# A key projection moved ahead of the scores, another projection behind the maxima's transposes, and context pieces loaded one batch earlier

## The chip, the cores and the metric

One NeuronCore of one Trainium2 chip runs the kernel; everything is float32. The metric is the device time of one execution in microseconds (us), taken as the median of several runs. The engines are named as the profile names them: PE (TensorE, the matmuls), PEld (its weight loads), DVE (VectorE), ACT (ScalarE), POOL (GpSimd) and SP (the queue that issues the DMAs).

## What is computed

A Perceiver-like block over `x` of 32 batches x 64 rows x 256, with a context of 32 x 1601 x 256:

```python
x = x + cross_attention(layernorm(x), ctx, ctx, mask)   # 16 heads of 16, softmax over 1601 keys
x = x + span_attention(layernorm(x))                    # softmax of -soft * (pos - mean)^2 over 64 rows
x = x + ffn(layernorm(x))                               # shared gated product + 2 of 8 experts per row
```

The cross attention makes nearly all of the work: for every batch the keys and values of 1601 context rows are projected (256 x 256 each), scores of 16 heads are formed against 64 queries, masked, made into a softmax with its true maximum, and multiplied with the values.

## The kernel before

**Units of work.** A batch's heads are handled in two *halves* of eight heads; half number n is batch b = n // 2, c = n % 2, and there are 64. The loop at line 767 runs over n and overlaps four things that belong to different halves: the scores of half n+1, the softmax of half n, the products with the values of half n-1, and the projection of the keys and values of batch b+1. The 1601 keys are cut into 13 blocks of 124. Context comes in four pieces (`GROUPS`: blocks 0-3, 4-6, 7-9, 10-12; five buffers `ct`, line 146), and scores in three *bursts* (`SCORED`: 4, 5 and 4 blocks).

**Operations of one half, as they stand in the loop.**
- `values(n-1, r)` (line 636, tile `pvs`): 104 small matmuls for r = 0, and 104 for r = 1. r = 0 needs the exponentials of pairs 0 and 1 of half n-1, r = 1 those of pairs 2 and 3.
- `exponentials(n, j)` (line 626, ACT, 124 x 1664): one for each of the four pairs of heads. The fourth, of pair 3, is written in the following half: `exponentials(n-1, 3)` at line 789, ahead of `scores(n+1, 0)`.
- `scores(n+1, g)` (line 549, tile `psc`): a burst into four banks (five for g = 1). DVE adds the mask on the way out (lines 566 and 573) and keeps running maxima (line 590; the first of them is an ACT copy, line 582, `mrun`).
- The maxima of half n: `turned_maxima` transposes them on PE (line 597, tile `pm`, behind the first burst of scores), DVE reduces them (line 604, tile `mc`, between its second and third addition of that burst), `maxima_along_rows` broadcasts them on PE (line 612, tile `pb`), and ACT copies them out (line 616, tile `mb`).
- `less_maxima(n, j)` (line 621, POOL): subtracts `mb` from each of the four pairs, 124 x 1664 each. The exponential of a pair needs it.
- `project_keys(b+1, c, g)` (tile `pk`, copied out by ACT at line 510 with the bias) for the four pieces g, and `project_values(b+1, u)` (tile `pv`, copied out by ACT at line 527) for seven units u of two blocks (the last of one). `tiled` splits a product into strips of 32 output columns (line 495), which leaves the sum of the work as it is.
- Small steps of the query projection and of the span attention are fed in by `run(...)` from an agenda; a set of them serves two batches, so four halves make one round.

**What sets the order.** PE, DVE, ACT and POOL execute their instructions in the order in which the code writes them (`manual_schedule`, line 733), each engine waiting at the head of its queue; SP issues DMAs in written order as well. Nearly all PE outputs of the loop come from one pool of six PSUM banks (`ps_x`, line 395, tag `mm`), which are taken in turn: a tile gets the bank of the tile six allocations before it, and its first matmul waits until that tile has been read out. In the kernel before, the allocations from the first burst on are `psc` x4, `pm`, `pk` of piece 0, `pb`, then those of the steps, `psc` x5, `pk` of piece 1, and so on.

`load_context(b+1)` (line 483) issues all four pieces of the next batch, and an `x` tile for even b, at the start of half c = 0.

Of the kernel before, what the change touches and what calls it, by code (L numbers as in the profile page):

```python
# [33 lines left out]
GROUPS = [(0, 4), (4, 3), (7, 3), (10, 3)]  # L34
# [56 lines left out]
def perceiver_kernel(ctx: ExitStack, tc: tile.TileContext, a: dict[str, bass.AP], out: bass.AP):  # L91
    nc = tc.nc
    B = a["ctxT"].shape[0]
    NT = B * S
    NTILE = NT // P
# [12 lines left out]
    def mm_bank(name: str):  # L108
        return ps_mm.tile([P, 512], F32, tag="mm", name=name)
# [16 lines left out]
    def load_x(t: int):  # L126
        xs[t] = work.tile([P, D], F32, tag="x", bufs=5, name=f"x{t}")
        nc.sync.dma_start(out=xs[t], in_=a["x"][t * P : (t + 1) * P, :])
# [14 lines left out]
    def load_piece(b: int, g: int):  # L143
        c0, n = GROUPS[g]
        k0, kn = c0 * CHUNK, min(n * CHUNK, KEYS - c0 * CHUNK)
        ct = big.tile([P, 2, 4 * CHUNK], F32, tag="ct", bufs=5, name=f"ct_{b}_{g}")
        nc.sync.dma_start(
            out=ct[:, :, :kn],
            in_=a["ctxT"][b].rearrange("(c p) k -> p c k", p=P)[:, :, k0 : k0 + kn],
        )  # L150
        cts[b].append(ct)
# [269 lines left out]
    def pair_of(n: int, j: int):  # L421
        return prob[:CHUNK, place(n, j // 2), j % 2]

    def block_of(n: int, k: int):

        first, last = place(n, 0), place(n, 1)
        return prob[:CHUNK, first : last + 1 : last - first, :, k, :]
# [52 lines left out]

        nc.gpsimd.tensor_tensor(xs[t], xs[t], bo_row, ALU.add)

    def load_context(b: int):
        for g in range(len(GROUPS)):
            load_piece(b, g)
        if b % 2 == 0 and b // 2 + 1 < NTILE:
            t = b // 2 + 1
            load_x(t)


    def product(out, lhsT, rhs, start: bool, stop: bool, tiled: bool):
        n = lhsT.shape[-1]
        for at in range(0, n, 32) if tiled else (0,):
            end = min(at + 32, n) if tiled else n
            nc.tensor.matmul(  # L495
                out[at:end], lhsT=lhsT[:, at:end], rhs=rhs, start=start, stop=stop,
                **(dict(tile_position=(0, at)) if tiled else {}),
            )
# [15 lines left out]
    def project_values(b: int, u: int, tiled: bool = False):  # L514

        blocks = range(2 * u, min(2 * u + 2, NKC))
        ps = mm_bank(f"pv_{b}_{u}")
        for n, k in enumerate(blocks):
            g = max(g for g in range(len(GROUPS)) if GROUPS[g][0] <= k)
            k0, kn = (k - GROUPS[g][0]) * CHUNK, min(CHUNK, KEYS - k * CHUNK)  # L520
            for i in range(2):
                product(
                    ps[:kn, n * D : (n + 1) * D], cts[b][g][:, i, k0 : k0 + kn], wvT[:, i, :],
                    i == 0, i == 1, tiled,
                )
        n = len(blocks)
        nc.scalar.copy(  # L527
            vs[b % 2][:kn, 2 * u : 2 * u + n, :, :DK],
            ps[:kn, : n * D].rearrange("p (n h d) -> p n h d", n=n, d=DK),
        )  # L530

    def scores(n: int, g: int, then=None, order=None):

        b, c = halves[n]
        c0, nb = SCORED[g]


        more = [mm_bank(f"psc_{b}_{c}_{g}"), spare_pvs] if nb == 5 else None
        pss = [mm_bank(f"psc_{b}_{c}_{g}_{j}") for j in range(4)]
        for r in range(nb):  # L540
            for j in range(4):
                e, s = divmod(j, 2)[::-1]
                fifth = nb == 5 and r == 4 * s
                i = 4 if fifth else r - (nb == 5 and s == 0)
                ps, at = (more[e], s) if fifth else (pss[j], i)
                if fifth and j == 2:
                    tc.add_manual_dep(nc.tensor.nop().ins, mm.ins.name, IN_TURN, reason="banks")
                k0 = (c0 + i) * CHUNK
                product = nc.tensor.matmul(  # L549
                    ps[:CHUNK, at * P : (at + 1) * P],  # L550
                    lhsT=kTs[c][32 * j : 32 * j + 32, k0 : k0 + CHUNK],
                    rhs=qbd[b // 2][32 * j : 32 * j + 32, c, b % 2, :, :],
                    start=True, stop=True, tile_position=(32 * j, 0),
                )
                if fifth and j == 1:
                    mm = product
        held = then() if then else None
        for item in (order or ORDER[g]).split():
            if item == "t":
                if held is not None:  # L560
                    maxima_of_rows(*held)
            elif item[0] == "m":
                maximum(n, int(item[1:]))
            elif item in "AB":
                k, e = c0 + 4, "AB".index(item)
                nc.vector.tensor_tensor(  # L566
                    block_of(n, k)[:, :, e, :],
                    more[e][:CHUNK, : 2 * P].rearrange("p (r q) -> p r q", r=2),
                    madd_fifth[:CHUNK, None, :].to_broadcast([CHUNK, 2, P]), ALU.add,
                )  # L570
            else:
                j = int(item)
                nc.vector.tensor_tensor(  # L573
                    pair_of(n, j)[:, c0 : c0 + 4, :].rearrange("p k (e q) -> p k e q", e=2),
                    pss[j][:CHUNK].rearrange("p (k e q) -> p k e q", k=4, e=2),
                    madd[:CHUNK, c0 : c0 + 4, None, :].to_broadcast([CHUNK, 4, 2, S]), ALU.add,
                )
# [6 lines left out]
    def maximum(n: int, k: int):  # L584

        dst = mrun
        if k == NKC - 1:
            dst = mxs[n] = work.tile([P, 4, P], F32, tag="mx", bufs=1, name="mx")
        dst, run = (m[:CHUNK].rearrange("p (r i) q -> p r i q", r=2) for m in (dst, mrun))
        nc.vector.tensor_tensor(dst, block_of(n, k), run, ALU.max)  # L590
# [11 lines left out]
    def maxima_of_rows(ps, col):  # L602

        nc.vector.tensor_reduce(  # L604
            col, ps[:, : 4 * CHUNK].rearrange("p (j k) -> p j k", j=4), AX.X, ALU.max
        )
# [18 lines left out]
    def exponentials(n: int, j: int):  # L625
        nc.scalar.activation(pair_of(n, j), pair_of(n, j), AF.Exp)  # L626
# [134 lines left out]
    next(queries, None)  # L761
    for u in range(7):
        project_values(0, u)
    last = len(halves) - 1

    extra = {3 * last - 3: (0,), 3 * last - 2: (1, 2, 4), 3 * last - 1: (5, 6)}
    for n, (b, c) in enumerate(halves[:-1]):
        if c == 0 and b + 1 < B:
            load_context(b + 1)
        if c and b % 2 == 0 and b // 2 + 1 < NTILE:  # L770
            agenda[3 * n].append((b // 2 + 1, query_steps(b // 2 + 1)))

        def project(f, *args):
            if b + 1 < B:
                f(b + 1, *args)

        def steps(g: int):
            run(3 * n + g)
            for u in extra.get(3 * n + g, ()):
                linear_factor(u)  # L780

        def taken_off():
            turned.extend(turned_maxima(n))
            return turned

        turned: list = []
        if n:
            values(n - 1, 0)
            exponentials(n - 1, 3)
        scores(n + 1, 0, taken_off)  # L790
        project(project_keys, c, 0)
        m = maxima_along_rows(turned[1])
        less_maxima(n, 0, m, nc.gpsimd)
        held = 3 * n in held_at
        if not held:
            first_maxima(n + 1)
        run(3 * n)
        if n:
            values(n - 1, 1)
            if c == 0:  # L800
                agenda[3 * n + 1].append((b // 2, finish_steps(b - 1, 3 * n + 1)))
        for u in extra.get(3 * n, ()):
            linear_factor(u)
        if held:
            first_maxima(n + 1)
        else:
            for k in (1, 2) if c else (1, 2, 3):
                maximum(n + 1, k)

        scores(n + 1, 1, order=LATER if held else None if c else SOONER)  # L810
        exponentials(n, 0)
        project(project_keys, c, 1)
        for u in (4, 5) if c else (0, 1):
            project(project_values, u)
        less_maxima(n, 1, m, nc.gpsimd)
        steps(1)
        exponentials(n, 1)

        less_maxima(n, 2, m, nc.gpsimd)
        scores(n + 1, 2)  # L820
        project(project_keys, c, 2, True)
        project(project_keys, c, 3, True)
        for u in (3, 6) if c else (2,):
            project(project_values, u, True)
        less_maxima(n, 3, m, nc.gpsimd)
        exponentials(n, 2)
        steps(2)
# [176 lines left out]
```

## Time and profile before

| | us |
|---|---|
| median of 3 runs (1519.32, 1520.34, 1524.4) | 1520.34 |
| span of the profiled execution, first to last instruction | 1515.7 |
| PE busy / POOL busy in it | 1465.0 / 1120.7 |
| DVE busy / ACT busy in it | 1225.5 / 946.9 |
| first `pm` of the loop to the last | 41.04 to 1347.68 |
| one `less_maxima` on POOL / one `exponentials` on ACT (means) | 3.75 / 1.59 |
| one copy of keys out of `pk` (124 to 496 columns, mean) | 0.585 |

The profiled execution's own time is its span; the profile holds no other time of it, and the median of the separate runs lies 4.6 us above the span. Busy time is the union of an engine's instructions; matmuls overlap, so a busy PE may still be held up inside. Idle time is put down to the instruction whose semaphore came last.

### The profile page before, as it was taken

To read this page: it belongs to the slowest core of one execution; us is meant where nothing else is said; L and a number is where in the kernel's file an instruction comes from. 1 tells how busy PE (TensorE), PEld (TensorE's weight loads), DVE (VectorE), ACT (ScalarE), POOL (GpSimd) and SP (SyncE) were. 2 spreads that over 40 slices of the span, in tenths; PEclk is the share of its full clock that TensorE was granted. 3 is DMA by queue.
4 is the path that set the end of the run, shared out by engine and by line. 5 is a ranking of instruction groups with operands and counts; after the bars stand their busy time and mean duration, and the time that the engine had idled before them with its cause. 6 is when DMAs were issued, how large, how long until landed. Compare 5 with 4: busy or idle time off the path is not lost.

```text
span 1515.7 us, 62949 instructions
## 1 busy us (share of the span) xinstructions
PE 1465.0 (97%) x28600; PEld 1066.5 (70%) x28600; DVE 1225.5 (81%) x2332; ACT 946.9 (62%) x1727; POOL 1120.7 (74%) x508
## 2 busy tenths in 40 slices
PE   8999999999999999999999999999999999998899
PEld 5677767777777767777777777676777677654587
DVE  4889898998989898989989898988899898873100
ACT  3565657676767657576766677575767566766411
POOL 1777787888878887878888888878788788852710
PEclk9999999999999999999999999999999999999999
DMA  5111111111111101111111111011111111005200
GB/s 174 37 45 46 46 47 46 36 50 50 50 50 50 49 25 41 47 53 37 49 50 50 50 50 49 24 43 46 54 37 48 50 50 33 3 9 160 60 29 29
DMA packets 52076, 73.82 MB, mean 49 GB/s; under 512 B 3812, under 2 KB 51040, under 8 KB 51680
## 3 DMA queue, kind: packets, MB, share of 16 engines
q1 hardware_dynamic: 50992, 69.00, 14.9%
q8 instruction: 225, 3.69, 1.0%
q10 hardware_dynamic: 816, 0.79, 0.2%
q14 instruction: 43, 0.35, 0.1%
HBM read 65.57 MB, written 4.19 MB: 46 GB/s over the span
## 4 chain that ended last, share of the span: by engine, by line
PE 76%; DVE 17%; ACT 4%; issue 2%; POOL 0%; DMA 0%; ACTq 0%; DVEq 0%; POOLq 0%
PE pk L495 20%; PE pv L495 19%; PE psc L549 10%; PE pvs L636 10%; DVE mrun L590 8%; DVE prob L573 6%; PE py L934 4%; PE pm L597 2%; PE u L665 2%; PE ph L916 2%; PE pb L612 2%; ACT qbd L474 1%; PE psa L357 1%; PE pq L466 1%; PE po L377 1%
## 5 line engine op out<-in xcount | busy, mean ns | idle before, releaser
L621 POOL TENSOR_TENSOR prob<-prob,mb 124x1664 f32<-124x1664 f32 x252 | 939.0, 3751 | 224.2 <-ACT mb L616 218.8
L573 DVE TENSOR_TENSOR prob<-psc,madd 124x512 f32<-124x512 f32 x768 | 504.0, 680 | 76.5 <-PE psc L549 76.0
L626 ACT ACTIVATE prob<-prob 124x1664 f32<-124x1664 f32 x256 | 406.9, 1591 | 185.0 <-POOL prob L621 182.0
L590 DVE TENSOR_TENSOR mrun<-prob,mrun 124x512 f32<-124x512 f32 x704 | 486.7, 691 | 33.9 <-ACT mrun L582 20.1
L495 PE MATMUL pk<-ct,wkT_sb 128*32 128x372 f32 (+1 forms) x2512 | 387.6, 489 | 8.9 <-DMA wkT_sb<-in_wkT 5.5
L495 PE MATMUL pv<-wvT_sb,ct 128*124 128x256 f32 x3524 | 381.0, 379 | 0.9 <-DVE prob L566 0.8
L495 PEld LDWEIGHTS pv<-wvT_sb,ct 128*124 128x124 f32 x3524 | 272.8, 132 | 110.4 <-issue 17.5
L549 PE MATMUL psc<-qbd,kT 32*124 32x128 f32 x6400 | 241.8, 279 | 8.3 <-issue 6.9
L495 PEld LDWEIGHTS pk<-ct,wkT_sb 128*32 128x32 f32 (+1 forms) x2512 | 148.9, 127 | 140.1 <-issue 95.5
L549 PEld LDWEIGHTS psc<-qbd,kT 32*124 32x124 f32 x6400 | 201.9, 181 | 41.8 <-issue 20.8
L636 PE MATMUL pvs<-prob,v 124*17 124x64 f32 x13312 | 213.6, 220 | 3.0 <-issue 2.8
L527 ACT COPY v<-pv 124x512 f32<-124x512 f32 (+1 forms) x224 | 124.5, 556 | 146.5 <-PE pv L495 146.1
L636 PEld LDWEIGHTS pvs<-prob,v 124*17 124x17 f32 x13312 | 196.0, 98 | 27.9 <-issue 15.7
L510 ACT ACTIVATE kT<-pk,cols 128x372 f32<-128x372 f32 (+2 forms) x256 | 145.7, 585 | 70.0 <-PE pk L495 69.7
L323 ACT ACTIVATE sc<-sc,least 128x64 f32<-128x64 f32 x256 | 85.8, 343 | 2.6 <-DVE least L319 2.5
L936 DVE SCALAR_TENSOR_TENSOR ot<-py,prob 128x256 f32<-128x256 f32 x16 | 6.8, 424 | 75.7 <-PE py L934 66.1
L665 PE MATMUL u<-xfT,sw_sb 128*128 128x512 f32 x128 | 60.9, 624 | 3.6 <-ACT prob L692 2.7
L582 ACT COPY mrun<-prob 124x512 f32<-124x512 f32 x64 | 38.2, 596 | 37.3 <-DVE soft L306 34.3
L612 PEld LDWEIGHTS pb<-cst,mc 128*124 128x124 f32 x256 | 29.4, 135 | 36.6 <-DVE mc L604 30.0
L549 PE MATMUL pvs<-qbd,kT 32*124 32x128 f32 x256 | 54.9, 294 | 0.0
L597 PE MATMUL pm<-cst,mx 124*128 124x124 f32 x256 | 41.4, 283 | 11.4 <-DVE mx L590 10.1
L323 ACT ACTIVATION_READ_ACCUMULATOR sc<-sc,least 128x1 f32 x256 | 49.9, 195 | 0.0
(126 smaller groups left out, 1220.3 us busy)
## 6 DMA issues: line engine op xcount, KB each, us to landing
ct<-in_ctxT SPq DMA_DIRECT2D x64, 372.0 KB, 3.2
ct<-in_ctxT SPq DMA_DIRECT2D x32, 496.0 KB, 5.1
ct<-in_ctxT SPq DMA_DIRECT2D x32, 361.0 KB, 3.9
w<-in_w SPq DMA_DIRECT2D x16, 256.0 KB, 7.0
x<-in_x SPq DMA_DIRECT2D x16, 128.0 KB, 2.1
x_kept<-x SPq DMA_DIRECT2D x16, 128.0 KB, 2.0
prob<-x_kept SPq DMA_DIRECT2D x8, 256.0 KB, 6.3
out<-ot SPq DMA_DIRECT2D x16, 128.0 KB, 1.9
```

The costliest lines, as they stand in the source:

```text
L323: nc.scalar.activation(sc[:, h, :], sc[:, h, :], AF.Exp, bias=least[:, h : h + 1], scale=-1.0, accum_out=total[:, h : h + 1],)
L495: nc.tensor.matmul(out[at:end], lhsT=lhsT[:, at:end], rhs=rhs, start=start, stop=stop, **(dict(tile_position=(0, at)) if tiled else {}),)
L510: nc.scalar.activation(kTs[c][:, k0 : k0 + kn], ps[:, :kn], AF.Identity, bias=cols[:, B_K + c : B_K + c + 1])
L527: nc.scalar.copy(vs[b % 2][:kn, 2 * u : 2 * u + n, :, :DK], ps[:kn, : n * D].rearrange("p (n h d) -> p n h d", n=n, d=DK),)
L549: product = nc.tensor.matmul(ps[:CHUNK, at * P : (at + 1) * P], lhsT=kTs[c][32 * j : 32 * j + 32, k0 : k0 + CHUNK], rhs=qbd[b // 2][32 * j ...
L573: nc.vector.tensor_tensor(pair_of(n, j)[:, c0 : c0 + 4, :].rearrange("p k (e q) -> p k e q", e=2), pss[j][:CHUNK].rearrange("p (k e q) -> ...
L590: nc.vector.tensor_tensor(dst, block_of(n, k), run, ALU.max)
L597: nc.tensor.transpose(ps[:, j * CHUNK : (j + 1) * CHUNK], m[:CHUNK, j, :], ident[:CHUNK, :CHUNK])
L621: engine.tensor_tensor(sj, sj, m[:CHUNK, j, None, :].to_broadcast([CHUNK, NKC, P]), ALU.subtract)
L626: nc.scalar.activation(pair_of(n, j), pair_of(n, j), AF.Exp)
L636: nc.tensor.matmul(pvs[32 * j : 32 * j + DK + 1, c, :, r, :], lhsT=v[:kn, k, 8 * c + h, :], rhs=pair_of(n, h // 2)[:kn, k, (h % 2) * S : ( ...
L665: nc.tensor.matmul(ps, lhsT=w[:, c, hc * P : (hc + 1) * P], rhs=xfT[:, c, :, slot], start=(c == 0), stop=(c == 1),)
```

## The change

Three edits in the loop. (1) The keys' piece 0 is projected ahead of the first burst of scores, tiled, instead of behind it untiled. (2) Behind the transposes of the maxima stands another unit: for c = 0 the keys' piece 1, for c = 1 the unit 3 of the values. The units after it move up accordingly: piece 2 of the keys goes from the third part of the half (tiled) to the second (untiled), and unit 5 of the values from the second part (untiled) to the third (tiled). (3) The four pieces of a batch are no longer issued together at c = 0 of the batch before it; each is issued one batch earlier still, behind the work that frees its buffer. The pieces of batch 1 are issued ahead of the loop.

```diff
-    def load_context(b: int):
-        for g in range(len(GROUPS)):
+    def piece_ahead(b: int, g: int):
+        if b < B:
             load_piece(b, g)
-        if b % 2 == 0 and b // 2 + 1 < NTILE:
-            t = b // 2 + 1
-            load_x(t)
...
+    for g in range(len(GROUPS)):
+        load_piece(1, g)
     last = len(halves) - 1
...
-        if c == 0 and b + 1 < B:
-            load_context(b + 1)
+        if c == 0:
+            piece_ahead(b + 2, 0)
+            if b % 2 == 0 and b // 2 + 1 < NTILE:
+                load_x(b // 2 + 1)
...
         if n:
             values(n - 1, 0)
             exponentials(n - 1, 3)
+        project(project_keys, c, 0, True)
+        if c:
+            piece_ahead(b + 2, 1)
         scores(n + 1, 0, taken_off)
-        project(project_keys, c, 0)
+        if c:
+            project(project_values, 3)
+        else:
+            project(project_keys, c, 1)
         m = maxima_along_rows(turned[1])
         less_maxima(n, 0, m, nc.gpsimd)
...
         scores(n + 1, 1, order=LATER if held else None if c else SOONER)
         exponentials(n, 0)
-        project(project_keys, c, 1)
-        for u in (4, 5) if c else (0, 1):
-            project(project_values, u)
+        if c:
+            project(project_keys, c, 1)
+            piece_ahead(b + 2, 2)
+            project(project_values, 4)
+            project(project_keys, c, 2)
+            piece_ahead(b + 2, 3)
+        else:
+            project(project_keys, c, 2)
+            for u in (0, 1):
+                project(project_values, u)
         less_maxima(n, 1, m, nc.gpsimd)
...
         less_maxima(n, 2, m, nc.gpsimd)
         scores(n + 1, 2)
-        project(project_keys, c, 2, True)
         project(project_keys, c, 3, True)
-        for u in (3, 6) if c else (2,):
+        for u in (5, 6) if c else (2,):
             project(project_values, u, True)
         less_maxima(n, 3, m, nc.gpsimd)
         exponentials(n, 2)
```

## The prediction

> **What bounds the kernel now.** I read the page first (busy time, slices, clock), then the waits of each engine, then one half of the loop in the timeline.
>
> ```profile
> span 1515.7 us, 62949 instructions
> PE 1465.0 (97%) x28600; PEld 1066.5 (70%) x28600; DVE 1225.5 (81%) x2332; ACT 946.9 (62%) x1727; POOL 1120.7 (74%) x508
> PE   8999999999999999999999999999999999998899
> ...
> PEclk9999999999999999999999999999999999999999
> ```
>
> PE is busy all through the loop, at full clock. What an edit there can gain is what PE waits for; what it can lose is a wait that PE does not have yet. The waits:
>
> ```profile
> PE pm L597 <- DVE mx L590: 10.1, 16, 2.4
> ...
> PE pb L612 <- DVE mc L604: 2.6, 3, 1.5
> ```
>
> ```profile
> ACT prob L626 <- POOL prob L621: 182.0, 108, 3.4
> ```
>
> ```profile
> POOL prob L621 <- ACT mb L616: 218.8, 62, 10.0
> ```
>
> So PE loses 12.7 us to the two steps of the maxima that the change covers (10.1 + 2.6); that is nearly all that it can win. The other two rows are a second ring: ACT waits for POOL's subtractions, and POOL waits once in every half (62 times) for `mb`. From `mb` to `mb` POOL has four subtractions of 3.75 us (15 us) and some small steps, so this ring is not far from binding. Half 33 in the timeline (start, duration, engine, line, operation):
>
> ```profile
> 700.51 0.58 ACT L616 COPY mb<-pb 124x512 f32<-124x512 f32 x1
> ...
> 701.17 3.74 POOL L621 TENSOR_TENSOR prob<-prob,mb 124x1664 f32<-124x1664 f32 x1 [2.51 <-ACT mb L616]
> ...
> 706.73 11.14 POOL L621 TENSOR_TENSOR prob<-prob,mb 124x1664 f32<-124x1664 f32 x3
> ...
> 716.78 0.64 PE L597 MATMUL pm<-cst,mx 124*128 124x124 f32 x4 [0.21 <-DVE mx L590]
> ...
> 717.26 1.83 PE L495 MATMUL pk<-ct,wkT_sb 128*128 128x496 f32 x4
> ...
> 717.91 1.59 ACT L626 ACTIVATE prob<-prob 124x1664 f32<-124x1664 f32 x1 [1.74 <-POOL prob L621]
> ...
> 718.92 0.60 PE L612 MATMUL pb<-cst,mc 128*124 128x128 f32 x4
> ...
> 719.40 0.66 ACT L510 ACTIVATE kT<-pk,cols 128x496 f32<-128x496 f32 x1
> ...
> 719.96 0.58 ACT L616 COPY mb<-pb 124x512 f32<-124x512 f32 x1
> ...
> 720.32 1.65 PE L636 MATMUL pvs<-prob,v 124*17 124x64 f32 x104
> ```
>
> The reader is to see one thing: the fourth exponential (717.91 to 719.50) starts when POOL ends its fourth subtraction (717.87), after `pm`, and the copy of keys comes behind it in ACT's queue. PE does not notice: its next unit (717.26) needs a bank that an older copy has freed.
>
> **The change, part by part.**
>
> *Piece 0 ahead of the burst.* The product moves by itself at no cost. Untiled it holds PE 1.66 us (717.26 to 718.92). Tiled, pieces 2 and 3 take 2.49 us for 733 columns (709.63 to 712.12), so 496 columns take 1.68. It stands between two kinds of small tile, as the values did; the switch is paid once either way. But its bank: of six banks in turn, piece 0 takes one, the burst four, `pm` the sixth, and the unit behind `pm` gets piece 0's bank back. That unit now waits for ACT's copy of piece 0, and the copy is written behind `exponentials(n-1, 3)`, which waits for POOL. The built order shows both: the unit's wait is on the copy of that same half's piece 0, with the fourth exponential ahead of it on ACT. Before, the unit waited for a copy that stood ahead of the fourth exponential. So PE takes on a new wait, in each half from 1 to 61. Behind it on PE stand `pb`, the step products and the values; behind `pb` ACT's `mb` and POOL; behind `mb` on ACT `mrun`, for which DVE's maxima wait. The ring POOL, ACT, PE, ACT closes once per half.
>
> Length of the ring from the end of one `mb` to the next. First to the end of the fourth subtraction, from the timeline, where the order on POOL is unchanged: 16.78 us to half 33 (701.09 to 717.87), 17.59 to half 34 (720.54 to 738.13), 16.30 to half 35 (741.19 to 757.49), 16.82 to half 36 (762.47 to 779.29). They differ by the small steps; four halves make a round. Then: start of the exponential 0.04, itself 1.59, the copy 0.56 more (719.50 to 720.06), PE's start 0.06 (as `pm` behind `mx`: 716.72 to 716.78), the unit, and from `pb` to the end of `mb` 1.24 (1.35 in half 32, less 0.11 for the shorter copy ahead of it). The unit is 1.36 for piece 1 (the same product from cold: 703.64 to 705.00) and 1.8 for values unit 3 (half of 705.00 to 708.54). Together 4.85 in even halves, 5.29 in odd.
>
> Against the distances in the trace: half 33: 16.78 + 5.29 = 22.07 against 19.45 (+2.62). Half 34: 17.59 + 4.85 = 22.44 against 20.65 (+1.79). Half 35: 21.59 against 21.28, but PE alone is longer there: 19.91 from `pb` (739.06) to `pm` (758.97) without a wait, 0.42 for piece 0 in place of piece 2, 0.48 for `pm`, 1.8 for the unit: 22.61 (+1.33; part of it is work that the next half is spared). Half 36: 21.67 by the ring, 21.87 by PE; I take 21.8 against 21.76. Sum 88.9 against 83.1: +5.8 a round, 15.25 rounds in 61 halves: **+88 us**. Lower end: only halves 33 and 34 gain, 4.41 x 15.25 = +67. Upper end: ACT reaches the fourth exponential late, as in the trace of halves 34 and 36 (738.58 after 738.13, 779.89 after 779.29); that is 1.05 a round, +104. I keep 88, because PE's third part of a half gets 1.26 us shorter, so the copies ahead of those exponentials come earlier.
>
> *Another unit behind `pm`, units moved up.* Work is conserved (the same columns; 733 tiled columns of keys become 857, tiled being no dearer). `pb` finds `mc` ready whenever the new wait is long; where it is short (half 36), piece 1 is 0.3 us shorter than piece 0 and `mc` was only 0.4 us ahead of `pb` (718.52 and 718.92): nothing, to +0.3 x 15 = 5 us. DVE gets the first burst 1.68 us later and the third part of PE's half is 1.26 shorter, so `mx` has 0.42 us more before `pm`. The 12.7 us of waits go, but inside the ring's slack; they are no further gain.
>
> *The clock.* PE reaches the unit 17.94 us after `pb` in half 33 (17.04 in the trace, 0.42, 0.48) and may start at 20.27: 2.3 us idle; 18.89 and 21.08 in half 34: 2.2. The tail shows what such a gap can do:
>
> ```profile
> 1344.76:1348.17 3.41, 0.98 (x40) 1.00 0.02 5
> 1348.17:1355.00 6.83, 6.06 (x113) 0.50 0.01 4
> ...
> 1399.37:1402.79 3.42, 1.40 (x4) 1.00 0.00 0
> 1402.79:1406.20 3.41, 0.00 (x0) 1.00 0.00 0
> ```
>
> (Stretch, length, PE busy, granted clock.) A stretch of 3.41 us with 2.43 idle was followed by half clock, one with 2.02 idle was not. A gap of 2.2 to 2.9 us (the upper value without the waits that PE still has on the way) falls into one such stretch in some rounds and is split in others. With some 30 gaps, and 1.7 us lost by a stretch of 3.41 at half clock, the bounds are 0 and 52 us; I take a quarter, 14, as a gap must nearly fill the stretch. The Trainium skill ("TensorE: Matmul & The Clock Gate", section "Why this matters for your kernels") asks for no idle gaps over about 3 us, by which these gaps would cost nothing and the sum would be 14 less; the row with 2.43 us speaks against it.
>
> *DMA and SP.* The same 128 pieces are issued. SP runs in order and often waits there for PE (lines L147, L128, L382); PE never waits for a piece in the loop. A piece lands 3.2 to 5.1 us after its issue and now has about a half (20 us) or more, because its buffer comes free with the projection named one line above the issue. `load_x` moves behind one piece in place of four, and what stood behind it (a piece at 761.32, after the `x` of 759.17) is now free of it. Cost nothing; without that cover up to 5.1 us for a piece.
>
> Sum against the execution's own 1515.7: 1515.7 + 88 + 14 = 1617.7, and with the 4.6 us by which the median lies above it **1622 us**.
>
> **Rivals.**
> *Faster: the new wait does not bind.* If exponential and copy ended before `pm`, PE would save the 12.7 us and lose up to 5 for `pb`: 1508 to 1516. It turns on where the fourth exponential ends: with 0.62 us for the copy and PE's start, against 0.48 for `pm`, it must be 0.14 us before `pm` starts or earlier. Halves 32 and 36 come nearest (698.42 and 781.49, 0.8 us after `pm` at 697.59 and 780.73); against it speak 719.50, 740.16 and 760.62, which lie 2.7, 3.3 and 1.7 us after theirs.
> *The ring binds in two halves of four only,* the rest drowning in slack: +67, no loss of clock: 1587.
> *The clock falls after nearly every gap:* 1515.7 + 88 + 52 + 4.6 = 1660.
> *Pieces come late:* SP held by an `x` or `x_kept` that waits (up to 16.3 us in the trace); at 5 us for each of 31 batches 155 us on top. Against it: 20 us of lead.
>
> **How the numbers follow.** Ring with some loss of clock, 1595 to 1645: 0.66, and the time is its 1622. Ring in two halves: 0.13. Clock always: 0.13. Late pieces: 0.03. No binding: 0.05, shared 0.03 faster and 0.02 the same. The range 1582 to 1655 leaves out the last two and most of the clock's worst. A difference of 0.3% (4.6 us) is about what a measurement can tell. Faster 0.03, same 0.02, slower 0.95.
>
> **What would show it.** Right: a new row in which PE's unit behind `pm` (`pk` and `pv`) waits for the ACT copy `kT`, about 60 us or more in total, longest 2 to 3 us; POOL's share of the loop near that of a bound engine; `pm` no longer waiting for `mx`; distances of `pm` near 22 us in all halves; stretches of half clock inside the loop. Wrong: `pk` or `pv` waiting for a `ct` transfer, the unit starting right behind `pm`, or PE's busy share still at 97% with a span near 1515.

## The result, and the profile after

The changed kernel takes 1645.8 us (median of 4 runs, 1641.9 to 1646.2) against 1519.8 for the kernel before beside it: ratio 1.083, 95% interval 1.079 to 1.086. It is 126 us slower; the prediction was 1622, with a range of 1582 to 1655. The profiled execution has a span of 1643.8 us.

The page of the changed kernel, as before (PE by slices left out):

```profile
span 1643.8 us, 62916 instructions
...
PE 1517.4 (92%) x28600; PEld 1088.9 (66%) x28600; DVE 1226.8 (75%) x2332; ACT 953.8 (58%) x1727; POOL 1120.0 (68%) x508
...
PEclk9999999999899999999998999999999999998899
```

ACT, POOL and DVE do the same work in nearly the same busy time as before (ACT takes 7 us more, the others differ by no more than 1.3). PE has more busy time for the same matmuls, 1517.4 against 1465.0, and the granted clock is below full in slices inside the loop. PE's waits in the changed kernel (engine, line, waited for: us in total, times, longest):

```profile
PE pk L492 <- ACT kT L507: 49.5, 30, 2.6
PE pv L492 <- ACT kT L507: 38.5, 16, 2.7
...
PE pm L594 <- DVE mx L587: 6.1, 16, 2.4
```

The first two rows did not exist before: 88 us, in 46 waits. The wait for `mx` has shrunk from 10.1 to 6.1 us. And ACT waits for POOL more often, 153 times in place of 108:

```profile
ACT prob L623 <- POOL prob L618: 253.4, 153, 3.4
```

The ring of half 41 in the timeline of the changed kernel (start, duration, engine, line, operation, and in brackets the idle time before it and who ended it):

```profile
946.71 0.58 ACT L613 COPY mb<-pb 124x512 f32<-124x512 f32 x1
947.37 3.73 POOL L618 TENSOR_TENSOR prob<-prob,mb 124x1664 f32<-124x1664 f32 x1 [3.09 <-ACT mb L613]
...
952.91 11.16 POOL L618 TENSOR_TENSOR prob<-prob,mb 124x1664 f32<-124x1664 f32 x3
...
962.98 0.61 PE L594 MATMUL pm<-cst,mx 124*128 124x124 f32 x4 [0.22 <-DVE mx L587]
...
964.11 1.59 ACT L623 ACTIVATE prob<-prob 124x1664 f32<-124x1664 f32 x1 [2.11 <-POOL prob L618]
965.61 0.66 ACT L507 ACTIVATE kT<-pk,cols 128x496 f32<-128x496 f32 x1
...
966.31 1.99 PE L492 MATMUL pv<-wvT_sb,ct 128*124 128x256 f32 x8 [2.72 <-ACT kT L507]
968.14 0.60 PE L609 MATMUL pb<-cst,mc 128*124 128x128 f32 x4
968.83 0.58 ACT L613 COPY mb<-pb 124x512 f32<-124x512 f32 x1
```

POOL's last subtraction ends at 964.07; the exponential, the copy of piece 0, the unit of values, `pb` and `mb` follow one another link by link, and PE stands still from 963.59 to 966.31 in front of a product whose inputs are all there.

For the rest one table does most of the work. It is read off the timelines of all runs with a profile: the mean distance in us from the end of one `mb` to the end of the next, in halves 2 to 61, by the place of the half in its round (half number modulo 4), and the sum of a round. The part from `mb` to POOL's fourth subtraction is the same in every run, within 0.05 us: 16.57, 16.67, 17.50 and 16.00 us.

| | place 0 | 1 | 2 | 3 | round |
|---|---|---|---|---|---|
| before | 21.45 | 19.52 | 20.53 | 21.34 | 82.8 |
| predicted, without the clock (halves 33 to 36) | 21.8 | 22.07 | 22.44 | 22.61 | 88.9 |
| changed | 21.44 | 22.66 | 23.49 | 23.33 | 90.9 |
| e4, gap filled with products | 21.45 | 22.10 | 22.45 | 22.50 | 88.5 |
| e9, gap filled by a quarter | 21.44 | 22.74 | 22.89 | 22.58 | 89.6 |
| e2, change with the old loads | 21.45 | 22.61 | 23.81 | 23.25 | 91.1 |
| e3, only the loads | 21.37 | 19.52 | 20.62 | 21.29 | 82.8 |
| e1, copy before the exponential | 20.68 | 19.48 | 20.87 | 22.18 | 83.2 |
| e5, piece 0 before the steps | 20.88 | 19.53 | 20.61 | 21.62 | 82.6 |
| e6, and the maxima reduced sooner | 20.53 | 19.60 | 20.60 | 22.31 | 83.0 |
| e7, only the unit behind | 20.86 | 20.83 | 20.71 | 22.43 | 84.8 |
| e8, only piece 0 ahead | 22.76 | 20.93 | 21.99 | 23.46 | 89.1 |

### The profile page after: what moved, and what is told of

Same layout as the page of the kernel before. It is cut to its first block, busy times and chain, and to the rows that moved or that the text cites. A ratio compares the mean times of both kernels' runs of the same rounds, so it can differ in the third digit from the quotient of the medians.

```text
span 1643.8 us, 62916 instructions
## 1 busy us (share of the span) xinstructions
PE 1517.4 (92%) x28600; PEld 1088.9 (66%) x28600; DVE 1226.8 (75%) x2332; ACT 953.8 (58%) x1727; POOL 1120.0 (68%) x508
## 4 chain that ended last, share of the span: by engine, by line
PE 38%; POOL 37%; ACT 18%; DVE 5%; issue 1%; DMA 1%; ACTq 0%; DVEq 0%; POOLq 0%
POOL prob L618 33%; PE pv L492 11%; ACT prob L623 8%; PE pk L492 8%; PE pvs L633 3%; PE py L947 3%; PE psc L546 3%; ACT kT L507 3%; PE u L662 2%; ACT sc L323 2%; PE ph L929 2%; DVE prob L570 2%; POOL sc L316 1%; DVE mrun L587 1%; PE pb L609 1%; ACT qbd L474 1%
## 5 line engine op out<-in xcount | busy, mean ns | idle before, releaser
L492 PE MATMUL pk<-ct,wkT_sb 128*32 128x496 f32 (+1 forms) x2512 | 412.9, 525 | 57.6 <-ACT kT L507 49.5
L492 PE MATMUL pv<-wvT_sb,ct 128*124 128x256 f32 x3524 | 397.1, 383 | 40.2 <-ACT kT L507 38.5
L546 PE MATMUL psc<-qbd,kT 32*124 32x128 f32 x6400 | 237.6, 279 | 1.7 <-ACT qbd L474 0.9
L507 ACT ACTIVATE kT<-pk,cols 128x372 f32<-128x372 f32 (+2 forms) x256 | 149.6, 584 | 96.0 <-PE pk L492 95.6
L380 DVE TENSOR_TENSOR x<-x,po 128x256 f32<-128x256 f32 x16 | 6.7, 421 | 71.1 <-PE po L377 71.1
L609 PEld LDWEIGHTS pb<-cst,mc 128*124 128x124 f32 x256 | 36.9, 157 | 20.2 <-issue 10.5
```

The lines of the kernel that those rows point to most:

```text
L492: nc.tensor.matmul(out[at:end], lhsT=lhsT[:, at:end], rhs=rhs, start=start, stop=stop, **(dict(tile_position=(0, at)) if tiled else {}),)
L507: nc.scalar.activation(kTs[c][:, k0 : k0 + kn], ps[:, :kn], AF.Identity, bias=cols[:, B_K + c : B_K + c + 1])
L546: product = nc.tensor.matmul(ps[:CHUNK, at * P : (at + 1) * P], lhsT=kTs[c][32 * j : 32 * j + 32, k0 : k0 + CHUNK], rhs=qbd[b // 2][32 * j ...
L609: nc.tensor.transpose(ps[:CHUNK, j * P : (j + 1) * P], col[:, j : j + 1].to_broadcast([P, CHUNK]), ident)
```

## The experiments

The theory: the unit behind `pm` waits for the bank of the same half's piece 0, whose copy stands on ACT behind the fourth exponential, which waits for POOL; this closes a ring, and on top of it the gap it leaves in PE costs clock. The rivals: the new places of the products on PE, the transfers, or a longer ring than thought without any clock in it.

### e1: the copy ahead of the exponential

```diff
             values(n - 1, 0)
-            exponentials(n - 1, 3)
         project(project_keys, c, 0, True)
+        if n:
+            exponentials(n - 1, 3)
```

> The changed kernel with one line moved: the projection of piece 0 (and with it its copy on ACT) is written ahead of the fourth exponential of the half before, not behind it. PE's order is that of the changed kernel. Theory (the unit behind pm waits for piece 0's bank, whose copy stands behind the fourth exponential and so behind POOL): the wait of pk and pv for the copy kT goes, the loop is bound by PE again as before the change and has lost the waits for the maxima: 1508 to 1522 us. Rival (the loss comes from the new places of the products on PE, from the transfers, or from POOL's load as such): stays over 1600 us.

Measured: 1524.1 us, ratio to before 1.0016 (1.0002 to 1.003). PE's order is untouched, and 122 us are gone with one line: the new places of the products, the transfers and POOL's load, all still there, do not make the loss. But the run lies 2 us above the expected 1508 to 1522. PE's waits of this run say why:

```profile
PE pk L492 <- ACT kT L507: 17.5, 13, 1.4
...
PE pb L609 <- DVE mc L601: 4.8, 16, 1.5
```

One wait of 1.1 to 1.4 us is left in most rounds, at place 2: at the start of that half ACT still has small steps (four exponentials of line 323 and two normalisations) in front of the copy.

### e2 and e3: the loads

e2 is the changed kernel with `load_context(b + 1)` at the start of c = 0 as before; e3 is the kernel before with each piece loaded behind the product that frees its buffer:

```diff
-        if c == 0 and b + 1 < B:
-            load_context(b + 1)
+        if c == 0:
+            piece_ahead(b + 2, 0)
+            if b % 2 == 0 and b // 2 + 1 < NTILE:
+                load_x(b // 2 + 1)
...
         project(project_keys, c, 0)
+        if c:
+            piece_ahead(b + 2, 1)
...
             project(project_values, u, True)
+        if c:
+            piece_ahead(b + 2, 2)
+            piece_ahead(b + 2, 3)
```

> The changed kernel with the context loaded as before (all four pieces of the next batch and the x tile at the start of half c = 0). Theory: the pieces' earlier loading plays no part, 1635 to 1655 us as the changed kernel. Rival (pieces held up on the queue, or transfers beside other work, make the loss): falls towards 1520 us.

> The kernel before with only the loading of the change: each piece is issued one batch earlier, behind the product that frees its buffer. Theory: hidden before and hidden now, 1515 to 1526 us. Rival (the loads make the loss): over 1560 us.

Measured: e2 1649.1 us, ratio 1.084 (1.082 to 1.087); e3 1520.8 us, ratio 1.0002 (0.9985 to 1.002). The third edit has no cost and no gain that these intervals can tell, alone or with the others (e2's interval overlaps with that of the changed kernel, 1.079 to 1.086).

### e4 and e9: products in PE's gap

```diff
         scores(n + 1, 0, taken_off)
+        if n % 4 in (1, 2):
+            for _ in range(4):
+                nc.tensor.matmul(
+                    spare_pvs, lhsT=wqT[:, 0, :P], rhs=wkT[:, 0, :], start=True, stop=True
+                )
```

(e9: one product in place of four.)

> The changed kernel with four products more (128 x 128 by 256 columns, about 1.7 us of PE, result not used) between pm and the unit behind it, in the two halves of each four where PE stands idle there for 2 to 2.7 us. Theory (about 34 of the 126 us are the clock, which halves after the gap): stretches of half clock in the loop go from 92 us to nearly nothing, the distance from mb to mb becomes 22.1, 22.5, 22.9 and 21.7 us, and the kernel gets faster by adding work: about 1610 us. Rival (the clock costs nothing since the ring waits anyway, or the ring is longer than thought for another reason): 1640 us or more, up to 1700 if the added products lie on the path.

> As the run with four products in PE's gap, but with one (about 0.4 us), so that some 1.8 to 2.3 us of each gap stay idle. In the profile of the changed kernel every stretch of 3.41 us of the loop with over 1.83 us idle was followed by half clock, of those between 1.71 and 1.83 some were, and none below. Theory (half clock follows a stretch of which more than about half is idle; the gap's whole length is not what counts): fewer stretches pass that mark, half clock in the loop 20 to 65 us in place of 92, 1615 to 1638 us. Rival (only a gap of some fixed length over 2.4 us counts, as the tail of the kernel before suggested): no half clock left, 1605 to 1612 us.

Measured: e4 1608.1 us, ratio 1.057 (1.055 to 1.059); e9 1625.6 us, ratio 1.070 (1.064 to 1.075). With 256 matmul instructions more the kernel is 38 us faster than the changed one. The clock row of e4 (each slice 40 us):

```profile
PEclk9999999999999999999999999999999999999899
```

Half clock inside the loop: 92 us in 17 places in the changed kernel (3.41 or 6.83 us each), none in e4, 44 us in 13 places of 3.41 us in e9. Between e4 and the other two the 60 halves of the table grow by 36 us and by 17: 0.39 us for each us at half clock in both cases. The added products do not lie on the path: the nine halves at place 1 of the changed kernel that ran at full clock throughout have 5.34 us behind POOL's fourth subtraction, and e4's have 5.42. So e4's distances are the ring without the clock. They are 22.10, 22.45, 22.50 and 21.45 us at places 1, 2, 3 and 0, where 22.1, 22.5, 22.9 and 21.7 were expected.

In e9 every stretch of 3.41 us of the loop with 1.98 us idle or more was followed by half clock; of the two between 1.85 and 1.95 one was (1.88), the other (1.91) not; none below. So a gap of fixed length over 2.4 us is not what counts: in e9 no gap in front of that unit was longer than 2.3 us, and 13 of them (2.1 to 2.3 us long) were still followed by half clock, where one stretch held most of the gap.

### e5 and e6: piece 0 earlier still

e5 is the changed kernel with the projection of piece 0 moved to the end of the half before, and one in front of the loop for half 0. e6 adds to that the order `"0 t 1 2 3"` in place of `"0 1 t 2 3"` for the first burst.

```diff
-        project(project_keys, c, 0, True)
         if c:
             piece_ahead(b + 2, 1)
...
         less_maxima(n, 3, m, nc.gpsimd)
         exponentials(n, 2)
+        ahead(n + 1)          # project_keys(b + 1, c, 0, True) of half n + 1
         steps(2)
```

> The changed kernel with the projection of piece 0 written earlier still: at the end of the half before, behind the third exponential and ahead of the small steps, so that its copy on ACT stands ahead of those steps and of the fourth exponential. In the run with one line moved, PE still waited 1.4 us a round for that copy, because ACT had small steps in front of it. Theory: that wait goes too (17.5 us in total), and PE-bound time is left: 1500 to 1512 us, faster than the kernel before. Rival (nothing is to be had over the kernel before, as the gain of the covered maxima is given back by pb waiting for mc or by the values starting later): 1515 to 1530 us.

> The kernel with piece 0 before the steps, and in addition DVE reduces the transposed maxima behind its first addition of the burst and not behind its second. Theory: pb, which waits for mc where piece 1 is shorter than piece 0 was (6.3 us in all in the run with one line moved), finds it ready: 4 to 7 us less than without this edit. Rival (DVE then holds the burst's banks longer, or waits for pm itself): no difference, or slower.

Measured: e5 1516.7 us, ratio 0.9969 (0.9952 to 0.9986): the only version faster than the kernel before, though by 4 us and not by the expected 8 or more; it lies in the range that the rival named (1515 to 1530). The wait for the copy is gone altogether. Of the small waits in PE's list two are longer than in e1, the one for `mc` (4.8 us there) and the one without a releaser (0.7 there):

```profile
PE pb L609 <- DVE mc L601: 7.0, 28, 1.5
...
PE pm L594 <- DVE mx L587: 5.6, 14, 2.4
...
PE psc L546 <- issue: 4.1, 10, 1.1
```

At place 0 a round gains 0.57 us over the kernel before, and at place 3 it gives back 0.28; why place 3 gets longer was not looked into. e6 missed: 1524.6 us, ratio 1.0021 (1.0006 to 1.0036). `pb` does find `mc` ready (1.6 us in place of 7.0), but another wait takes its place right behind `pb`, at the step product of line 377, and the one for `mx` grows:

```profile
PE po L377 <- ACT kT L507: 11.4, 12, 1.2
PE pm L594 <- DVE mx L587: 9.9, 17, 2.4
```

That PE, arriving sooner, merely meets the next bank that ACT has not read out is what the first row suggests; it does not explain that the sum got worse. The table puts the loss at place 3 (22.31 in place of 21.62); why stays open.

### e7 and e8: the first two edits, each alone

e7 leaves piece 0 behind the burst, untiled, and puts the other unit behind it; the units after it (piece 2 and unit 5) stay in their old places:

```diff
         scores(n + 1, 0, taken_off)
         project(project_keys, c, 0)
+        if c:
+            project(project_values, 3)
+        else:
+            project(project_keys, c, 1)
...
-        project(project_keys, c, 1)
+        if c:
+            project(project_keys, c, 1)
...
-        for u in (3, 6) if c else (2,):
+        for u in (6,) if c else (2,):
```

e8 only moves piece 0 ahead of the burst, tiled; `pb` follows `pm` directly.

> The kernel before with the second edit alone: piece 0 stays behind the burst and untiled, and the other unit follows it, ahead of the broadcast of the maxima (piece 1, or values unit 3). No unit there gets the bank of piece 0's copy of the same half. Theory: no ring, 1512 to 1532 us. Rival (any further product ahead of pb lengthens the way to mb and with it POOL's ring): over 1560 us.

> The kernel before with the first edit alone: piece 0 tiled and ahead of the burst, nothing between pm and pb. Now pb itself gets piece 0's bank and waits for its copy. Theory: the ring binds as in the changed kernel but without the unit in it (about 20.3 and 21.1 us in halves 1 and 2 of a round), and in halves 3 and 0 pb waits up to 1.65 us for mc, which nothing covers: 87 to 88 us a round and some half clock, 1580 to 1635 us. Rival (the wait needs the unit that follows): 1510 to 1530 us.

Measured: e8 1618.2 us, ratio 1.063 (1.059 to 1.067), inside the expected 1580 to 1635, with a round of 89.1 us (87 to 88 expected) and 7 us at half clock in the loop. `pb` now has both waits.

```profile
PE pb L612 <- DVE mc L604: 64.7, 44, 1.7
PE pb L612 <- ACT kT L510: 32.4, 20, 1.8
```

But e8 does not isolate the ring. With no product between `pm` and `pb` nothing covers DVE's reduction, and 65 of these 97 us are put down to `mc`. Even at places 1 and 2, where the theory had only the copy, `mc` comes last in 11 of 31 waits, and the two end close together: 2.19 us (copy) and 2.66 (`mc`) behind POOL's fourth subtraction at place 1, 2.92 and 2.81 at place 2 (medians). So these halves take 20.93 and 21.99 us and not the expected 20.3 and 21.1: at place 1 `mc` is the later one, and at place 2 ACT reaches the fourth exponential only 0.79 us after POOL's fourth subtraction (0.03 at place 1). An uncovered reduction of some 1.5 us in each of 60 halves would by itself make about 90 us (an estimate from these waits), so the time is no evidence for the ring. That it comes from the first edit is shown by e1, which alters nothing but the place of piece 0's copy in ACT's order, and by e7, which has a unit behind `pm` and no wait for a copy.

e7: 1550.5 us, ratio 1.019 (1.015 to 1.022), where 1512 to 1532 was expected. Neither side was right. PE has no wait for a copy of keys here; the loss is in another row of its waits:

```profile
PE pm L597 <- DVE mx L590: 44.3, 45, 2.4
```

The unit is taken from behind the second burst (piece 1, 1.35 us) or from behind the third (values unit 3, tiled, 1.73 us), so PE reaches the next `pm` that much sooner after the bursts, and DVE has that much less time for its maxima: 34 us more of this wait, for 30 us in the median. By this reading, which no run tests by itself, the two edits need each other: the first puts piece 0 (1.78 us tiled, as measured in the changed kernel) back in front of `pm` and pays for what the second takes away there, and the second covers the reduction that the first lays open.

## Why the prediction was right, and where it missed

*The new wait and its ring: right.* The row that was to appear is there, 88 us against "60 us or more", with 2.6 and 2.7 us as the longest against 2 to 3. The terms behind POOL's fourth subtraction are 4.87 us at place 0 and 5.34 at place 1, measured over the halves at full clock, against 4.85 and 5.29. e4 shows the ring without the clock: 1327.5 us for the 60 halves of the table against 1242.5 before, +85, against a predicted +88 for 61. Place by place (1, 2, 3, 0) it adds 2.58, 1.92, 1.16 and 0.00 us; 2.62, 1.79, 1.33 and 0.04 were predicted. Two of the signs that the prediction named did not come. POOL's busy share fell (from 74% to 68% of the span), since its four subtractions and small steps, 16.0 to 17.5 us of each distance, are only the first part of the ring. And the distances from `pm` to `pm` are 20.0, 23.7, 26.2 and 21.0 us at places 1, 2, 3 and 0, not near 22 in all halves: the ring sets the distance of `mb`, not of `pm`.

*That PE, not the ring, sets place 3: right.* 22.50 us in e4, 22.61 predicted, and in none of the halves at place 3 does PE wait for the copy.

*The clock: the mechanism was right, the size was off.* This is the term that carries the miss: 1645.8 lies inside the range, but just above the 1595 to 1645 of the case called likeliest. The prediction took 14 us out of bounds of 0 and 52 (a quarter of 52 is 13), "as a gap must nearly fill the stretch". The loop lost 36 us (changed kernel against e4; 38 in the medians), and 1622 with 36 in place of 14 would have been 1644. The spans grew by 128 us; the 7 us that are neither ring nor clock lie outside the 60 halves of the table. The failed step is the reading of the tail: from one stretch with 2.43 us idle that was followed by half clock and one with 2.02 that was not, it concluded that a gap has to be nearly as long as the stretch. In the loop, 17 of the 29 gaps of over 1.4 us at places 1 and 2 did it, none of them longer than 2.74 us.

*The maxima's waits: right that they are no further gain in the changed kernel* (the wait for `mx` went from 10.1 to 6.1 us, and the kernel got slower). But the rival "faster" promised 1508 to 1516 if the new wait did not bind, and e5, where it does not, reached 1517: of 12.7 us of waits it has 4 us. The prediction's bound for `pb` behind the shorter piece 1 (up to 5 us) was near: 7.0 us in e5 against 2.6.

*Transfers: right.* e2 and e3 show no cost and no gain. Two readings there were loose, without harm to the result: of the three lines named, only L147 waits for PE (L128 waits for ACT and L382 for DVE), and 3.2 to 5.1 us from issue to landing are medians by size of piece; the longest landing took 6.5.

*The rivals.* "Clock always" (1660) was nearer to the measured 1645.8 than its chance of 0.13 said; the truth lies between it and the likeliest case.

## What to carry to other kernels

When a product is moved on PE, its evacuation moves in another engine's queue: look up which tile will reuse its bank, and what stands ahead of the copy that frees it. An in-order engine passes on the lateness of whatever it has in front, here POOL's, to a product that has nothing to do with it; one line that put the copy first was worth 122 us. And a wait in PE costs more than its length once the clock reacts to it: price the gap and the clock apart, by filling the gap.

## What the runs showed of the hardware

The clock fell after shorter gaps than the tail of the kernel before suggested. Two neighbouring stretches of the changed kernel twice (stretch, length, PE busy, granted clock; the last two columns are the share and GB/s of the DMA):

```profile
869.03:872.44 3.41, 0.61 (x4) 1.00 0.33 104
872.44:875.86 3.42, 3.42 (x8) 0.50 0.02 5
1333.24:1336.65 3.41, 1.66 (x8) 1.00 0.02 5
1336.65:1340.07 3.42, 3.42 (x122) 1.00 0.00 0
```

With 2.80 us of 3.41 idle the next stretch ran at half clock, with 1.75 idle it did not. In the changed kernel every stretch of the loop with 1.83 us idle or more was followed by half clock, and of the 17 between 1.71 and 1.83 seven were, down to 1.72. In e2 one with 1.63 was followed by it and one with 1.84 was not, and in the tail of the kernel before one with 2.02 was not. So the mark lies near half of a stretch and is not sharp by these records. The stretches follow one another on a fixed grid (all starts of half clock in the changed kernel lie whole multiples of 3.413 us apart), so the same gap counts in one round and is split in the next: of the twelve gaps of 2.71 to 2.74 us at place 1, five were followed by half clock and seven were not. The Trainium skill ("TensorE: Matmul & The Clock Gate", section "Why this matters for your kernels") advises against idle gaps of over about 3 us; gaps of 2.7 us and less lost 36 us here, so the measurement decides against that figure.

Adding work made a kernel faster: 256 more matmul instructions, 38 us less. Only the four products, which left gaps of at most 1.1 us, helped fully; one product, a quarter of that, left 44 us at half clock.
